# A four-layer decoder on one core: VectorE and ScalarE put into a written order from the local transformer to the end of the first cross attention

## The chip, the core and the metric

The kernel runs on one core of one Trainium2 chip. TensorE multiplies matrices into PSUM; VectorE, ScalarE and GpSimd (called POOL in the profile) do the work on elements; SyncE issues most transfers. Each engine takes its instructions in the order of its own queue, and an instruction waits until the semaphores of what it needs have come. The metric is the time of one execution on the device in microseconds (us).

## The reference

The model is a decoder with layernorm after each part (post-norm), over 32 sequences of 64 tokens with 128 features: 2048 tokens, `x` of shape (32, 64, 128). There are four layers, each with self attention, cross attention to a context of the same shape, and a feed-forward part. Everything is in fp32. Cut to the parts that matter:

```python
x = layernorm(x + L0_attn(x))            # 16 heads of 8, rotary positions
x = layernorm(x + L0_xattn(x, ctx))      # two-way cross attention with a gate
x = layernorm(x + L0_ffn(x))             # "local transformer", two layers:
    #   h = shift_token(t); q, k, v = h @ wqkv        (8 heads of 64)
    #   q, k = rotary(l2norm(q) * qs), rotary(l2norm(k) * ks)
    #   t = t + softmax(8 q k^T, causal) v @ wo
    #   h = layernorm(shift_token(t)) * g + b
    #   t = t + (a * gelu(g)) @ w2 + b2,  a, g = split(h @ w1 + b1)
x = layernorm(x + L1_attn(x))            # "latent attention": 16 heads of 64, k and v from 64 latents
x = layernorm(x + L1_xattn(ctx, x, ctx)) # first plain cross attention, 16 heads of 8
x = layernorm(x + L1_ffn(x))             # 8 experts, tokens sorted by expert
x = layernorm(x + L2_attn(x)); x = layernorm(x + L2_xattn(x, ctx))
x = layernorm(x + L2_ffn(x))             # 8 experts with room for 80 tokens each
x = layernorm(x + L3_attn(x)); x = layernorm(x + L3_xattn(x, ctx)); x = layernorm(x + fp8_linear(x))
```

## The kernel before

The tokens are four blocks (`NBLK`) of 512, each block four tiles (`TPB`) of 128 tokens, that is, of two sequences. `x` stays in SBUF through all layers.

**The table of steps.** Nothing runs in loops on the chip. Each stage enters small functions into a table, `sp.at(step, place, f)`; `Steps.run` sorts by step and place and calls them, and so the program is written out. A stage has a base step: local transformer 23, latent attention 55, first cross attention (`l1x`) 71, its experts' tiles from 92, second self attention (`l2a`) 96, second cross attention (`l2x`) 112. Stages overlap in steps: a tile that starts in step k is scored in step k + 2 and leaves in step k + 4, while the next stage's tiles start.

**Whose order holds.** TensorE always takes its instructions in the table's order (`manual_schedule`, at the end of `decoder_kernel`). In the stretches of steps in `sp.fixed` VectorE and ScalarE do so too. Everywhere else, and always for POOL and the transfers, a planner orders the instructions at compile time by dependences and by the times that it reckons. It also picks the buffers. Before the change the fixed stretches are the steps 95 to 128 and 136 to 196.

**PSUM.** Tag S has two buffers of two banks, for `qkps` (queries and keys before rotation) and `s64`/`s8` (scores). Tag G has four single banks, for all else: transposes `ropeT`, `ptps`, `hnT` and `xTps`, values `v64`, attention output `o64`, projection `y64`, the feed-forward's `gps`, `aps` and `y2`, the latents `latps`. A TensorE instruction that writes a bank waits until the bank's last reader, mostly a ScalarE copy, is done.

**A tile of heads of 64** (`tiles64`; local transformer with 8 heads, latent attention with 16) goes through these functions; the profile's names are in brackets:
- `start`: TensorE projects (qkps, v). In the local transformer ScalarE squares (sq, L1125), VectorE sums the squares (rn, L1129), and POOL takes max (L1130) and the power -1/2.
- `rope`: VectorE makes three products (turn) out of qkps, one of full and two of half size (`rope64`; in the latent attention twice three); POOL adds them and, in the local transformer, multiplies by rn.
- `rotate`, two steps later: TensorE transposes (ropeT, L969), ScalarE copies (qk, L970).
- `score`: scores (s); VectorE takes the maximum (mx, L988) and subtracts (p); ScalarE takes the exponential (p, L992).
- `normal`: VectorE sums (rec, L998) and inverts (L999); the multiplication of p is VectorE's for 8 heads and POOL's for 16.
- `probs`: transposes (ptps, L1009), copies (pT, L1011). `values`: TensorE (o), copies (oT, L1027). `out`: projection (y); for every second tile VectorE adds the residual (`done`).

Around them the local transformer has, for each block and layer: `shifted` (the shifted input hT; two ScalarE copies and a POOL memset), `normed` (copies xs, statistics, POOL's rstd, and VectorE centres xs, L1173), `turn_h`, `hidden` (three pairs gps/aps, Gelu on ScalarE, L1196, products on VectorE, L1197) and `second` (y2; two POOL additions resid in layer 1; acc on VectorE; in layer 1 the layernorm). Counted in steps from the block's first tile, `shifted` is at -1, `normed` to `second` are at 7, 8, 9 and 10, so each falls on a fixed one of a block's four steps. ScalarE loads a table of functions (ACT_TABLE_LOAD) before the first Gelu and again before the next exponential.

A layernorm is `moments` (statistics and aggregates on VectorE, rstd on POOL) and `normed`; with `pool=False`, as at the ends of the local transformer and the latent attention, VectorE makes nb = -mean * rstd (L522) and ScalarE applies it with four activations (x, L515).

**Routing** (`routed`) goes by pieces of tokens, in the last steps of a cross attention: `logits`, `compare`, `choose`, `chosen`, `rows` (ranks; inc in the profile) and one indirect POOL transfer per tile (L1362). Then `tables` finds which rows each expert tile takes and issues 23 loads on SyncE's queue; for the experts with limited room `loads` issues three.

Of the kernel before, what the change touches and what calls it, by code (L numbers as in the profile page):

```python
# [20 lines left out]
P = 128  # L21
# [260 lines left out]
class Decoder:  # L282
# [392 lines left out]
    def attn8(self, sp, base, name, src=None, rope=None, scale=1.0, row=None, mask=(None, None), has_out=True, split=False, number=False, turned=None, ahead=None, held=False):  # L675
# [142 lines left out]
        for blk in range(NBLK):  # L818
# [5 lines left out]
            if halved(blk):  # L824
                sp.at(*((base + 16, 6.5) if turned is None else (base + 16, 5.8)), lambda blk=blk: turn(blk, (0, 2)))
                sp.at(*((base + 17, 6.5) if turned is None else (base + 17, 2.1)), lambda blk=blk: turn(blk, (2, 2)))
                sp.at(*((base + 16, 6.4) if turned is None else (base + 16, 5.3)), lambda: normal_rest(0))
                sp.at(*((base + 17, 6.4) if turned is None else (base + 17, 2)), lambda: normal_rest(1))
# [5 lines left out]
        for n in range(4 * NBLK):  # L834
            sp.at(base + n, 0, lambda n=n: score(n))
            sp.at(base + n, 6.5 if held or ahead else 0.01, lambda n=n: exps(n))
# [135 lines left out]
    def scores64(self, qT, kT, nh):  # L972
# [18 lines left out]
        p3 = pr.rearrange("p n u k -> p (n u) k")  # L991
        nc.scalar.activation(p3, p3, AF.Exp)  # L992
        return p3
# [37 lines left out]
    def tiles64(self, sp, first, n, project, twist, turn, nh, wo, done):  # L1031
# [18 lines left out]

        def normal(i):
            self.normal64(st[i][0], nh)
# [20 lines left out]
        for i in range(n):  # L1073
            for lag, place, f in (
                (2, 0, rotate), (0, 1, start), (2, 2, score), (0, 2.3, rope), (2, 2.6, normal), (3, 4, probs), (4, 5, out),
                (3, 6, values),
            ):
                sp.at(first + i + lag, place, lambda f=f, i=i: f(i))


    def local_transformer(self, sp, base, names):

        nc = self.nc
        cur, tabs = {}, []
# [27 lines left out]
        def project(i):  # L1112
# [14 lines left out]
            nc.scalar.copy(v, vp)  # L1127
            rn = self.sb([P, 16], "rn", 3)
# [3 lines left out]
            return (ps, rn), (v[:, 0], v[:, 1])  # L1132

        def twist(i, t):
            ps, rn = t
            tab = tabs[i // 16]
            full = lambda a: a.unsqueeze(2).to_broadcast([P, 2, 8, 64])
            t1 = self.rope64(ps, full(tab[:, :, 0, :]), full(tab[:, :, 1, :]))
# [20 lines left out]
        def normed(l, blk):  # L1159
# [8 lines left out]
            for t in range(TPB):  # L1168
                nc.vector.bn_stats(st[:, t, :], xs[:, t, :])
                nc.vector.bn_aggr(mv[:, t, :], st[:, t, :])  # L1170
            r = self.rstd(mv[:, :, 1], TPB)
# [29 lines left out]
        def second(l, blk):  # L1201
# [13 lines left out]
            else:  # L1215
                self.norm(blk, x2, pool=False)
# [3 lines left out]
        for l in range(2):  # L1220
            for blk in range(NBLK):
                n = base + 16 * l + 4 * blk
                for lag, place, f in ((-1, 7, shifted), (7, 7, normed), (8, 7, turn_h), (9, 7, hidden), (10, 3, second)):
                    sp.at(n + lag, place, lambda f=f, l=l, blk=blk: f(l, blk))
                if l:
                    sp.at(n + 12, 3, lambda blk=blk: self.turn_x(blk))


    def latent_attn(self, sp, base, name):
# [3 lines left out]
        lats, zs = {}, {}  # L1233
# [44 lines left out]
        def done(i, y):  # L1278
# [5 lines left out]
            if t == TPB - 1:  # L1284
                self.norm(blk, zs.pop(blk), pool=False)

        self.tiles64(sp, base, 16, project, lambda i, t: t, turn, 8, lambda i: self.w[name]["wo"], done)
        for blk in range(NBLK):
            sp.at(base + 4 * blk - 1, 7, lambda blk=blk: latent(blk))
# [654 lines left out]
```

## Time and profile before

| | us |
|---|---|
| median of 3 runs (lowest, highest) | 1421.75 (1417.74, 1424.29) |
| profiled execution | 1411.89 |
| its span | 1410.1 |
| TensorE matmul busy | 1201.6 |
| VectorE busy | 931.4 |
| POOL busy | 741.2 |
| ScalarE busy | 688.2 |

In time the stages lie so: first attention and gated cross attention to about 147 us; local transformer's tiles from 147 to about 517; latent attention to about 800, with the last feed-forward parts of the local transformer in its first half; first cross attention to 885; experts to 945; the third layer to 1190; the last to the end. The profile gives busy time by engine, the waits (who waited for whom, in total, how often, and the longest), the chain (work followed back from the last instruction by what released it), and a timeline. PE is TensorE, DVE VectorE, ACT ScalarE; L346 and L343 are the helpers of all element-wise operations on two tensors and of all matmuls, so there the tensors' names tell which it is.

### The profile page before, as it was taken

Reading aid. Unit: us, or ns where it says so; the run is one execution under the profiler, and the core shown is the slowest. Engines: PE = TensorE matmul, PEld = TensorE weight load, DVE = VectorE, ACT = ScalarE, POOL = GpSimd, SP = SyncE. Lnnn points to the kernel's source line nnn. Section 1 sums busy time; section 2 is a strip of 40 time slices with the busy share of each in tenths; the row PEclk is TensorE's granted clock in tenths of the full one; section 3 lists DMA queues with packets and bytes.
Section 4 is the critical chain, followed back from the end, with each engine's and each line's share of the span. In section 5 each row is a group of like instructions: output and inputs, shape, how many; then the busy total and the mean of one; then the engine's idle time right before and its main releaser. Section 6 shows DMA issues by size and latency. Waiting matters only on the chain.

```text
span 1410.1 us, 37014 instructions
## 1 busy us (share of the span) xinstructions
PE 1201.6 (85%) x16009; PEld 870.3 (62%) x16009; DVE 931.4 (66%) x1852; ACT 688.2 (49%) x1176; POOL 741.2 (53%) x619
## 2 busy tenths in 40 slices
PE   7998877898888878998898998697999948889991
PEld 4775455565655555666667777584678847567770
DVE  6764667777876776766666576554668743766796
ACT  2453445555555535454545553463656524345562
POOL 3533688766876674544454245352355443336543
PEclk9999999999999889999999998697999868889995
DMA  6001010180010000010001100220001100000001
GB/s 240 3 2 26 1 47 1 36 265 2 1 55 1 1 1 2 2 69 2 2 1 35 36 2 29 70 86 16 10 3 48 37 14 23 9 9 3 3 2 30
DMA packets 33715, 43.16 MB, mean 31 GB/s; under 512 B 5946, under 2 KB 27121, under 8 KB 33168
## 3 DMA queue, kind: packets, MB, share of 16 engines
q1 hardware_dynamic: 31536, 38.20, 8.5%
q0 software_dynamic: 2016, 2.60, 0.6%
q8 instruction: 126, 2.06, 0.6%
q14 instruction: 37, 0.30, 0.1%
HBM read 26.63 MB, written 15.56 MB: 30 GB/s over the span
## 4 chain that ended last, share of the span: by engine, by line
PE 53%; DVE 20%; POOL 12%; ACT 9%; issue 4%; DMA 2%; SPq 0%; POOLq 0%; ACTq 0%; DVEq 0%
PE s L343 11%; PE o L343 9%; DVE turn L346 5%; PE qkps L343 5%; PE ptps L669 5%; PE proj L343 5%; POOL turn L346 5%; PE y L343 3%; PE ropeT L969 3%; ACT pT L671 2%; DVE rn L1129 2%; DVE p L346 2%; POOL rstd L346 2%; PE hps L343 2%; POOL rn L346 2%
## 5 line engine op out<-in xcount | busy, mean ns | idle before, releaser
L346 POOL TENSOR_TENSOR turn<-turn,turn 128x1024 f32<-128x1024 f32 x64 | 150.6, 2361 | 95.8 <-DVE turn L346 85.9
L656 DVE TENSOR_REDUCE mx<-s 128x16 f32<-128x1024 f32 x96 | 117.3, 1222 | 110.2 <-PE s L343 110.1
L346 DVE TENSOR_TENSOR p<-s,mx 128x1024 f32<-128x1024 f32 (+1 forms) x144 | 159.0, 1104 | 6.0
L671 ACT COPY pT<-ptps 128x512 f32<-128x512 f32 x192 | 103.5, 588 | 76.7 <-PE ptps L669 75.8
L726 ACT ACTIVATE p<-p 128x1024 f32<-128x1024 f32 x96 | 101.4, 1056 | 54.3 <-DVE p L346 54.1
L343 PE MATMUL s<-kx,q 32*64 32x128 f32 x3072 | 111.7, 284 | 7.4 <-DVE sparts L1725 3.7
L346 DVE TENSOR_TENSOR turn<-qkps,w_const 128x512 f32<-128x512 f32 (+1 forms) x96 | 75.9, 861 | 57.1 <-PE qkps L343 57.1
L440 POOL TENSOR_SCALAR rstd<-bnmv 128x4 f32<-128x4 f32 (+1 forms) x60 | 16.0, 266 | 183.8 <-DVE bnmv L489 158.1
L343 PEld LDWEIGHTS s<-kx,q 32*64 32x64 f32 x3072 | 87.6, 138 | 39.2 <-issue 33.3
L669 PE MATMUL ptps<-w_const,p 128*128 128x128 f32 x768 | 107.3, 284 | 0.7 <-ACT p L726 0.5
L969 PE MATMUL ropeT<-w_const,turn 128*128 128x128 f32 x512 | 70.2, 284 | 29.5 <-ACT oT L1027 12.6
L346 POOL TENSOR_TENSOR rn<-rn,nhalf 128x16 f32<-128x16 f32 x32 | 93.8, 2930 | 2.7
L669 PEld LDWEIGHTS ptps<-w_const,p 128*128 128x128 f32 x768 | 88.5, 146 | 9.9 <-issue 8.4
L594 POOL TENSOR_TENSOR kx<-k,w_const 128x1024 f32<-128x1024 f32 x31 | 59.1, 1927 | 65.5 <-ACT k L603 31.4
L343 PEld LDWEIGHTS o<-v,pT 128*64 128x64 f32 x2176 | 72.5, 139 | 32.3 <-ACT pT L671 16.0
L343 PE MATMUL o<-v,pT 128*64 128x18 f32 x2176 | 81.0, 214 | 5.4 <-ACT pT L671 4.2
L969 PEld LDWEIGHTS ropeT<-w_const,turn 128*128 128x128 f32 x512 | 58.5, 144 | 41.1 <-ACT oT L1027 11.8
L346 DVE TENSOR_TENSOR turn<-qkps,xtab 128x512 f32<-128x512 f32 (+1 forms) x96 | 82.0, 859 | 0.0
L343 PE MATMUL o<-pT,v 64*64 64x64 f32 x2048 | 71.6, 223 | 8.9 <-ACT pT L1011 8.9
L509 POOL TENSOR_SCALAR x<-z,bnmv,rstd 128x128 f32<-128x128 f32 x98 | 77.8, 806 | 2.5
L1129 DVE TENSOR_REDUCE rn<-sq 128x16 f32<-128x1024 f32 x32 | 39.0, 1217 | 57.6 <-ACT sq L1125 57.6
L343 PE MATMUL qkps<-wbig,hT 128*128 128x512 f32 x128 | 67.9, 657 | 10.4 <-POOL hT L1105 9.1
(345 smaller groups left out, 2791.3 us busy)
## 6 DMA issues: line engine op xcount, KB each, us to landing
sorted_x<-zero SPq DMA_DIRECT2D x9, 990.0 KB, 14.5
wbig<-in_l1f_w_dram SPq DMA_DIRECT2D x4, 1156.0 KB, 5.3
wbig<-in_l2f_w_dram SPq DMA_DIRECT2D x16, 256.0 KB, 2.8
wbig<-in_l0f_dram SPq DMA_DIRECT2D x2, 1561.0 KB, 8.5
z<-token_y SPq DMA_DIRECT2D x8, 256.0 KB, 2.8
wbig<-in_l1a_dram SPq DMA_DIRECT2D x1, 1856.0 KB
xsorted<-sorted_x SPq DMA_DIRECT2D x23, 66.0 KB, 1.8
xT<-in_xT_dram SPq DMA_DIRECT2D x4, 256.0 KB, 6.4
```

The lines of the kernel that those rows point to most:

```text
L343: self.nc.tensor.matmul(out, lhsT=lhsT, rhs=rhs, start=start, stop=stop)
L346: (eng or self.nc.vector).tensor_tensor(out=out, in0=a, in1=b, op=op)
L440: nc.gpsimd.tensor_scalar(r[:, :n], var, EPS, None, ALU.add)
L509: eng.tensor_scalar(x[:, t0 + t, :], z[:, t0 + t, :], mv[:, t, 0:1], r[:, t : t + 1], ALU.subtract, ALU.mult)
L594: self.wide = eng.tensor_tensor(out=kx, in0=bc(kT, 1, 2), in1=bc(head[:, 2 * i : 2 * i + 2], 2, TB), op=ALU.mult).ins
L656: nc.vector.tensor_reduce(mx, s3, AX.X, ALU.max)
L669: self.nc.tensor.transpose(ps[:, j, :], flat[:, c : c + P], self.ident)
L671: self.nc.scalar.copy(o, ps)
L726: nc.scalar.activation(prs[n], prs[n], AF.Exp)
L969: self.nc.tensor.transpose(pt[:, j * P : (j + 1) * P], f[:, j * P : (j + 1) * P], self.ident)
L1129: nc.vector.tensor_reduce(rn, sq, AX.X, ALU.add)
```

## The change

It adds the fixed stretch of steps 29 to 88, and lengthens the next by one step (95 to 129). The local transformer's first six steps (23 to 28) stay with the planner. In the new stretch VectorE and ScalarE follow the table, so the functions are given new places in a step and some are cut in two:
- `tiles64`: `normal` goes from the end of `score`'s step to place 0.5 of the next step; `rope` goes ahead of `score`; the exponential becomes a function of its own, `exps`, at 6.5, behind the copies of `values`.
- local transformer: rn (sum, max, power) moves from `project` into `twist`, behind the turn products. `normed` ends with rstd; the centring is a new function, `centred`, at 0.6 of the next step. The layernorm at the end of layer 1 splits into `moments`, in `second`, and `ended` at 6.6. The latent attention's layernorm splits the same way.
- first cross attention: the exponential goes to 6.5, where the later attentions have it. For both routed cross attentions the last half block's normalization and transpose go to 4.06 and 4.07, and the pieces of tokens 12 to 15 to other places. `tables` and `loads` go to place 0 of the step after.

TensorE's order changes only by this last point.

```diff
-                sp.at(*((base + 17, 6.5) if turned is None else (base + 17, 2.1)), lambda blk=blk: turn(blk, (2, 2)))
+                sp.at(*((base + 17, 4.07) if turned is None else (base + 17, 2.1)), lambda blk=blk: turn(blk, (2, 2)))
-                sp.at(*((base + 17, 6.4) if turned is None else (base + 17, 2)), lambda: normal_rest(1))
+                sp.at(*((base + 17, 4.06) if turned is None else (base + 17, 2)), lambda: normal_rest(1))
-            sp.at(base + n, 6.5 if held or ahead else 0.01, lambda n=n: exps(n))
+            sp.at(base + n, 6.5 if base else 0.01, lambda n=n: exps(n))
@@ scores64
-        p3 = pr.rearrange("p n u k -> p (n u) k")
-        nc.scalar.activation(p3, p3, AF.Exp)
-        return p3
+        return pr.rearrange("p n u k -> p (n u) k")
@@ tiles64
+        def exps(i):
+            nc = self.nc
+            nc.scalar.activation(st[i][0], st[i][0], AF.Exp)
-                (2, 0, rotate), (0, 1, start), (2, 2, score), (0, 2.3, rope), (2, 2.6, normal), (3, 4, probs), (4, 5, out),
-                (3, 6, values),
+                (2, 0, rotate), (3, 0.5, normal), (0, 1, start), (0, 1.5, rope), (2, 2, score), (3, 4, probs), (4, 5, out),
+                (3, 6, values), (2, 6.5, exps),
@@ local_transformer
+            return (ps, sq), (v[:, 0], v[:, 1])
+
+        def twist(i, t):
+            ps, sq = t
+            tab = tabs[i // 16]
+            full = lambda a: a.unsqueeze(2).to_broadcast([P, 2, 8, 64])
+            t1 = self.rope64(ps, full(tab[:, :, 0, :]), full(tab[:, :, 1, :]))
             rn = self.sb([P, 16], "rn", 3)
             nc.vector.tensor_reduce(rn, sq, AX.X, ALU.add)
             nc.gpsimd.tensor_scalar(rn, rn, 1e-24, None, ALU.max)
             self.tt(rn, rn, self.nhalf[:, 0:16], ALU.pow, nc.gpsimd)
...
-            r = self.rstd(mv[:, :, 1], TPB)
+            ff[l, blk] = xs, mv, self.rstd(mv[:, :, 1], TPB)
+
+        def centred(l, blk):
+            xs, mv, r = ff[l, blk]
             for t in range(TPB):
                 nc.vector.tensor_scalar(
...
-                self.norm(blk, x2, pool=False)
+                ends[blk] = x2, self.moments(blk, x2)
+
+        def ended(blk):
+            x2, moments = ends.pop(blk)
+            self.normed(blk, x2, moments, False)
...
-                for lag, place, f in ((-1, 7, shifted), (7, 7, normed), (8, 7, turn_h), (9, 7, hidden), (10, 3, second)):
+                for lag, place, f in ((-1, 7, shifted), (7, 7, normed), (8, 0.6, centred), (8, 7, turn_h), (9, 7, hidden), (10, 3, second)):
+                    sp.at(n + 10, 6.6, lambda blk=blk: ended(blk))
@@ latent_attn
-                self.norm(blk, zs.pop(blk), pool=False)
+                ends[blk] = self.moments(blk, zs[blk])
+
+        def ended(blk):
+            self.normed(blk, zs.pop(blk), ends.pop(blk), False)
+            sp.at(base + 4 * blk + 7, 6.6, lambda blk=blk: ended(blk))
@@ routed
-            (12, 2, [(n + 9, 4)], (n + 9, 4.05), (n + 9, 6), (n + 9, 6.1), (n + 9, 6.2), [(n + 9, 6.3)] * 2),
-            (14, 2, [(n + 9, 7)], (n + 9, 7.1), (n + 9, 7.2), (n + 9, 7.3), (n + 9, 7.4), [(n + 9, 7.5)] * 2),
+            (12, 2, [(n + 9, 4)], (n + 9, 4.05), (n + 9, 4.6), (n + 9, 4.7), (n + 9, 4.8), [(n + 9, 4.9)] * 2),
+            (14, 2, [(n + 9, 4.5)], (n + 9, 4.51), (n + 9, 7.2), (n + 9, 7.3), (n + 9, 7.4), [(n + 9, 7.5)] * 2),
@@ sorted_experts, capacity_experts
-        sp.at(ready + 9, 8.1, tables)
+        sp.at(ready + 10, 0, tables)
-        sp.at(ready + 9, 8.1, loads)
+        sp.at(ready + 10, 0, loads)
@@ decoder_kernel
+    sp.fixed.append((29, n + 18))
-    sp.fixed.append((n - 1, n + 33))
+    sp.fixed.append((n - 1, n + 34))
```

More of the change, by code (lines that the diff above doesn't have):

```diff
@@ L1083, in local_transformer @@
         nc = self.nc
-        cur, tabs = {}, []
+        cur, tabs, ends = {}, [], {}
         def tables():
@@ L1131, in project @@
             self.tt(rn, rn, self.nhalf[:, 0:16], ALU.pow, nc.gpsimd)
[L1132 to L1138, printed above, removed]
             self.tt(t1, t1, bc(rn, 2, 64), ALU.mult, nc.gpsimd)
@@ L1169, in normed @@
                 nc.vector.bn_stats(st[:, t, :], xs[:, t, :])
+            for t in range(TPB):
                 nc.vector.bn_aggr(mv[:, t, :], st[:, t, :])
-            r = self.rstd(mv[:, :, 1], TPB)
+            ff[l, blk] = xs, mv, self.rstd(mv[:, :, 1], TPB)
+        def centred(l, blk):
+            xs, mv, r = ff[l, blk]
             for t in range(TPB):
@@ L1232, in latent_attn @@
         tab = self.c["r1"].rearrange("p (c s d) -> p c s d", c=2, d=64)
-        lats, zs = {}, {}
+        lats, zs, ends = {}, {}, {}
         def latent(blk):
```

## The prediction

> **What bounds it now.** I read the span and busy shares first, then the windows by stage, then waits and the chain of the stages that the change touches, last the timeline engine by engine. The profiled execution took 1411.89 us (span 1410.1, 1.8 around it); it lies 9.9 below the median of the runs shown, 1421.75. I sum against 1411.9 and carry the difference over to the median.
>
> ```profile
> PE 1201.6 (85%) x16009; PEld 870.3 (62%) x16009; DVE 931.4 (66%) x1852; ACT 688.2 (49%) x1176; POOL 741.2 (53%) x619
> ```
>
> No engine is full, so waits between engines set the time. By windows, the local transformer (147 to 521 us) has TensorE busy 83 to 86%, the latent attention (521 to 800) 252 of 279 us, the steady part of the first cross attention (804 to 862) 55.4 of 58. What can be won lies in the first two.
>
> In the local transformer the longest waits (window 147 to 520; columns: us in total, times, longest) form a ring:
>
> ```profile
> POOL rn L1130 <- DVE rn L1129: 78.9, 27, 5.1
> ACT p L992 <- DVE p L346: 62.8, 28, 3.5
> DVE rn L1129 <- ACT sq L1125: 57.6, 25, 7.4
> ```
>
> The chain shows one turn of it (start us, us, what):
>
> ```profile
> 305.34 1.22 DVE rn L1129
> 306.56 1.13 DVE turn L346
> 307.69 0.60 DVE mx L988
> 308.29 0.60 DVE turn L346
> 308.88 0.61 DVE p L346
> 309.50 0.02 issue
> 309.52 0.06 ACT p L992
> 309.58 0.48 issue
> 310.05 0.58 ACT pT L1011
> 310.63 0.04 issue
> 310.68 1.15 PE o L343 x32
> 311.82 1.02 PE ropeT L969 x8
> 312.85 1.73 PE qkps L343 x4
> ```
>
> Before rn lie qkps (302.53, 1.73 us) and ScalarE's squares sq (304.28, 1.03 us), so a tile takes 10.32 us. ScalarE keeps the exponential (p) ahead of the copy pT of an older tile, so TensorE waits for this tile's scores to pass through VectorE, though `o` doesn't need them.
>
> In the latent attention a plain step is TensorE's own (673.7 to 686.4: 12.67 us, nearly without gaps). Time is lost where a layernorm ends (timeline of ScalarE, then of TensorE: start, us, what, and in brackets the idle time before it and what ended it):
>
> ```profile
> 701.36 1.65 ACT L515 ACTIVATE x<-z,nb,rstd 128x128 f32<-128x128 f32 x4 [3.43 <-DVE nb L522]
> 702.91 0.56 ACT L1239 COPY lat<-latps 128x512 f32<-128x512 f32 x1
> ```
> ```profile
> 703.53 1.11 PE L969 MATMUL ropeT<-w_const,turn 128*128 128x128 f32 x4 [3.86 <-ACT lat L1239]
> 704.44 3.62 PE L343 MATMUL qkps<-wbig,xT 128*128 128x512 f32 x4
> ```
>
> TensorE stands 3.86 us for a PSUM bank that `lat` must empty, and the next qkps takes 3.62 us where 1.88 is usual: it restarts slow. VectorE's nb took 1.86 us there (others 0.16), beside POOL's multiplication of p.
>
> **The change, part by part.** TensorE's order in the tiles stays as it was. A tile's VectorE order becomes: normalize the older tile (reduce 0.71, reciprocal 0.24, multiply 1.28 to 1.93, I take 1.70: 2.65), three turn products (2.33), rn (1.14), mx and p (1.20). ScalarE's exponential (0.65) is last in its step, and next step's normalizing waits for it. A **plain local step** so becomes a VectorE ring of 2.65 + 2.33 + 1.14 + 1.20 + 0.65 = 8.0 us instead of 10.3; TensorE needs 7.3, POOL about 8.1.
>
> But a block of four tiles has more. I count from the normalizing in the step that ends with `hidden`:
> - Ring to p 7.3, exponential 8.0, Gelu table 9.25, first Gelu 9.9; the third gps/aps pair waits for it, 11.9; last product 12.7. The next normalizing now stands behind these products; before, it ran while the table loaded.
> - Step with `second`: TensorE runs on from 11.8: ropeT 0.9, qkps 1.8, v 1.0, s 0.95, y2 2.8, ptps and its copy 1.2, o 1.15, then oT: 22.5. The exponential's table load follows oT (before, it lay in ScalarE's wait for p): 1.28, then 0.65: 24.4.
> - Step with `normed`: 2.65 + 4.67 = 31.8 at p; exponential and the two xs copies to 33.2, statistics and aggregates 34.5.
> - Step with `centred`: normalizing 37.1, and rstd (POOL, 1.35) is hidden behind it if POOL is free, or comes at 38.9 behind a turn product (2.25); centred 1.05, ring, exponential: 43.5 to 45.3.
> Mean 44.4. The starts of qkps give 46.5, 45.8, 44.1, 44.1 now, mean 45.1. So only 0.7 a block, **3 us** for the four and a half plain blocks: what the ring wins, the uncovered tables and the Gelu products take back.
>
> Here the Trainium skill speaks against the change. The profile has the load before an exponential as
>
> ```profile
> 618.37 1.28 ACT L992 ACT_TABLE_LOAD   x1 [4.07 <-DVE p L346]
> 619.66 1.06 ACT L992 ACTIVATE p<-p 128x1024 f32<-128x1024 f32 x1
> ```
>
> so the function starts 1.29 us after it. "ScalarE: Activation LUTs", section What ACT_TABLE_LOAD costs, puts a switch at about 2.66 us, 1.38 of them a drain. Eight loads come out of cover: 10.3 us by the row, which is in my sums, 21.3 by the rule; the gain would be 11 smaller. I take the row.
>
> **The two blocks with the second layer's norm** took 53.2 and 56.0. There acc waits for POOL's two resid (2.4), then rstd behind POOL's turn products; ScalarE stands 6.1 and 4.8 us at x. Now acc, statistics and rstd are issued at `second`, and nb and x after the exponential. VectorE's nb now waits in order, and behind it the normalizing; ptps waits for that. If resid is early, rstd is there at the exponential and 7 us are won each. If POOL puts pow (2.9) and resid ahead, acc comes 5 us later and ScalarE's qk copies after it, and 1 is won. I take 3.5 each: **7 us**.
>
> **Latent attention.** At the norms of its blocks 0 to 2: z, statistics, aggregates, rstd without POOL's multiplication beside it, nb at 697.9, oT, exponential until 698.95, x (1.55), lat done 701.0 in place of 703.5. TensorE's gap shrinks from 3.9 to 1.5 us and the slow restart (1.74 + 0.35) goes: 4.6 each, **14 us**. Against it: the exponential (1.06) now lies between oT and the qk copies. In steps where the bank of y is still held (three of four left) the last ropeT waits for the first copy, 0.9 us, five times uncovered: **-4.5**. In the steps with `second` (at 545 and 609) the table and the exponential come ahead of x: about 1 and 3 later: **-4**. Two waits for rstd before `centred` lose POOL's multiplication ahead of them: **+2**.
>
> **First cross attention.** Only its exponential moves (to the end of its step); TensorE is full: **-1**, between -4 and +2. In both routed tails the turn of the last half block goes ahead of the ranks of the tokens before it. Eight scatters at 1.27 us each on POOL's queue follow from 879.6 and end the stretch, whatever comes for the last pair: the first of them comes 0 to 0.5 us earlier each: **+0.5**. `tables` (23 loads on SP, and weight copies) and `loads` (three) move past no work; they only leave the ordered stretch, which in the second tail is one step longer now. Splitting exponential, norm and centring adds no instruction. DMAs and POOL stay under the planner.
>
> Sum: 3 + 7 + 14 - 4.5 - 4 + 2 - 1 + 0.5 = 17 us. 1411.9 - 17 = 1394.9 for a profiled execution, **1405** for the median. Its own range: 1397 to 1412.
>
> **Rivals.**
> *VectorE behind POOL* (slower). POOL's order is still the planner's, and VectorE can no longer step aside. It waits in order at eight centred, four acc and eight nb: twenty places. Local steps have POOL 8.1 busy of 8 to 11 us. If rstd always comes behind a turn product, the centred cost 11 more than my mean; if resid and pow go ahead at the four norms of the local transformer, 5 each, 20: 31 against the gain of 17, 1421.75 + 14 = 1436. It decides from 0.85 us a place. For it: POOL's chain ran resid, turn, turn, rstd at 444 to 452. Against: the latent norms find POOL idle.
> *The exponential in the way* (no change). If the late exponential holds ropeT in all sixteen latent steps, it costs 17 instead of 4.5: 1417; with the tables at 2.66, 1421 or more. Against: with four banks free, qk copies aren't waited for.
> *The ring opens* (more). POOL takes rstd and resid early everywhere: blocks at 43.5 (4 more in sum), norm blocks 7 each (7 more), `second` without loss (4): 1390.
>
> **Chances.** Forecast 0.45, POOL 0.23, exponential 0.19, ring 0.13. What a measurement can tell from no change is 0.5%, 7 us: 1414.6 to 1428.9. Faster: 0.45 + 0.13, and a little of the third, 0.60; slower 0.23; same 0.17. The range of 8 in 10: 1391 at the low end, where the ring's case starts, 1432 at the high end, in the middle of POOL's.
>
> **What would show it.** Right: in the local transformer turn directly after qkps and before rn; plain steps of 8 to 8.5 us; table loads of the exponential directly after oT; x at the latent norms some 2.5 us earlier, and qkps after it at 1.9, not 3.6 us. Wrong: long waits of VectorE for POOL's rstd or resid, more than 1 us each; ropeT waiting for qk copies in every latent step; slow qkps in places that had none. The stretches from 945 us on should keep their lengths.

## The result and the profile after

The changed kernel takes 1485.69 us (median; 1484.22 to 1486.62), the kernel before beside it 1421.22. The ratio is 1.0445, 95% interval 1.0403 to 1.0486: by that ratio **slower by 63 us**, where 1405 was forecast. The profiled execution has a span of 1484.4 us against 1410.1, 74.3 more; the profiled execution of before lay 9 us below its median, this one 0.6 above.

First, by the starts of TensorE's qkps and of POOL's scatters, where the 74.3 us are:

| stretch | before | after | more |
|---|---|---|---|
| start to the first tile of the local transformer | 147.1 | 149.5 | 2.5 |
| its first six steps (planner's order) | 64.0 | 70.2 | 6.2 |
| its seventh tile to the end of its tiles | 306.2 | 351.7 | 45.5 |
| latent attention, first to sixteenth tile | 230.7 | 231.5 | 0.7 |
| from there to the first scatter | 101.2 | 116.7 | 15.6 |
| the sixteen scatters of the first routing | 39.5 | 45.6 | 6.1 |
| all the rest | 521.5 | 519.2 | -2.3 |

The busy row of the changed kernel:

```profile
PE 1229.2 (83%) x16009; PEld 880.8 (59%) x16009; DVE 913.4 (62%) x1852; ACT 688.8 (46%) x1176; POOL 735.6 (50%) x619
```

VectorE and POOL are busy for less time than before (931.4 and 741.2); TensorE has 28 us more for the same instructions. So no engine has more to do: there is new waiting, and TensorE's work got slower around it. The waits of the changed kernel in the local transformer (window 147 to 571 us; us in total, times, longest):

```profile
POOL turn L346 <- DVE turn L346: 127.1, 26, 9.0
...
DVE turn L346 <- ACT sq L1127: 66.7, 31, 8.7
DVE acc L346 <- POOL resid L346: 40.8, 6, 7.7
...
PE ropeT L969 <- DVE acc L346: 34.4, 6, 6.6
...
PE qkps L343 <- POOL hT L1107: 25.6, 7, 4.9
```

The ring that I had shown (rn for sq, p for p) is gone from the top. In its place turn waits for the squares, and two small POOL operations hold TensorE: resid, which acc needs, and the memset of hT, which qkps needs. The same two waits of TensorE before (window 147 to 520):

```profile
PE qkps L343 <- POOL hT L1105: 9.1, 5, 3.0
...
PE ropeT L969 <- DVE acc L346: 1.3, 1, 1.3
```

The chain of the changed kernel passes through a step with `second` like this (start, us, what):

```profile
430.46 1.03 ACT sq L1127
...
431.51 2.43 DVE turn L346 x3
...
434.08 2.36 POOL turn L346
436.44 0.23 POOL rn L1139
...
436.74 2.93 POOL rn L346
...
439.75 1.90 POOL turn L346
441.65 1.06 POOL resid L346
...
442.74 0.70 DVE acc L346
...
443.48 1.12 PE ropeT L969 x4
```

Nothing in resid depends on this tile: it adds a row to x1, which was there three steps ago. It only stands in POOL's queue behind the four operations of this tile's rotation, 7.5 us. What TensorE sees of it, and of the memset a step later (timeline of TensorE; in brackets the idle time before, and what ended it):

```profile
443.48 1.12 PE L969 MATMUL ropeT<-w_const,turn 128*128 128x128 f32 x4 [5.29 <-DVE acc L346]
444.39 3.62 PE L343 MATMUL qkps<-wbig,hT 128*128 128x512 f32 x4
...
459.44 3.78 PE L343 MATMUL qkps<-wbig,hT 128*128 128x512 f32 x4 [3.02 <-POOL hT L1107]
```

The second half of ropeT needs the fourth G bank, which y2 holds until acc has read it. After these two gaps qkps takes 3.6 to 3.8 us instead of 1.88, after all thirteen such gaps 2.4 to 3.8. In the kernel before, POOL's order in the same places was (timeline of POOL):

```profile
396.84 2.93 POOL L346 TENSOR_TENSOR rn<-rn,nhalf 128x16 f32<-128x16 f32 x1
399.74 1.09 POOL L346 TENSOR_TENSOR resid<-x,w_rows 128x512 f32<-128x512 f32 x1
400.79 2.36 POOL L346 TENSOR_TENSOR turn<-turn,turn 128x1024 f32<-128x1024 f32 x1
...
410.34 2.36 POOL L346 TENSOR_TENSOR turn<-turn,turn 128x1024 f32<-128x1024 f32 x1 [0.25 <-DVE turn L346]
412.75 0.11 POOL L1105 MEMSET hT<- 64x8 f32 x1
412.94 2.06 POOL L346 TENSOR_TENSOR turn<-turn,rn 128x1024 f32<-128x1024 f32 x1
```

There resid lies between the power and the addition, in all six blocks that have one in this stage; the memset lies between the addition and the multiplication in five of seven places. In the changed kernel both lie behind all four operations, everywhere.

In the first cross attention the loss has another form. The chain at its start:

```profile
816.15 1.51 PE s L343 x34
...
817.68 1.24 DVE mx L656
818.94 1.23 DVE p L346
820.17 1.14 DVE rec L996
821.33 0.26 DVE rec L997
...
821.75 1.91 POOL p L346
...
823.71 1.97 PE ptps L1007 x8
```

L656 is the maximum of the new attention's scores, which TensorE makes first in this step; rec (L996) is the normalization of a latent tile that was scored in the step before. VectorE takes them in this order, because the scores are at place 0 and the normalization at 0.5. So the old tile's transposes (ptps), in the middle of the step, wait for the scores of the same step, and the next scores come behind the transposes. Three steps, from scores to scores, take 18.7, 15.9 and 16.2 us that took 15.7, 10.7 and 9.6.

### The profile page after: what moved, and what is told of

Same layout as the page of the kernel before. It is cut to its first block, busy times and chain, and to the rows that moved or that the text cites. A ratio compares the mean times of both kernels' runs of the same rounds, so it can differ in the third digit from the quotient of the medians.

```text
span 1484.4 us, 37063 instructions
## 1 busy us (share of the span) xinstructions
PE 1229.2 (83%) x16009; PEld 880.8 (59%) x16009; DVE 913.4 (62%) x1852; ACT 688.8 (46%) x1176; POOL 735.6 (50%) x619
## 4 chain that ended last, share of the span: by engine, by line
PE 51%; DVE 19%; POOL 13%; ACT 10%; issue 4%; DMA 2%; SPq 0%; POOLq 0%; ACTq 0%; DVEq 0%
PE s L343 10%; PE o L343 8%; DVE turn L346 6%; PE qkps L343 6%; POOL turn L346 5%; PE proj L343 5%; PE ptps L669 4%; PE y L343 4%; POOL rn L346 4%; PE ropeT L969 3%; ACT pT L671 2%; DVE p L346 2%; PE ptps L1007 2%; ACT sq L1127 2%; DVE mx L656 1%
## 5 line engine op out<-in xcount | busy, mean ns | idle before, releaser
L656 DVE TENSOR_REDUCE mx<-s 128x16 f32<-128x1024 f32 x96 | 117.3, 1222 | 131.1 <-PE s L343 124.9
L671 ACT COPY pT<-ptps 128x512 f32<-128x512 f32 x192 | 103.6, 588 | 74.4 <-PE ptps L669 73.4
L969 PE MATMUL ropeT<-w_const,turn 128*128 128x128 f32 x512 | 74.2, 291 | 54.6 <-DVE acc L346 34.4
L346 DVE TENSOR_TENSOR turn<-qkps,xtab 128x512 f32<-128x512 f32 (+1 forms) x96 | 77.5, 861 | 66.7 <-ACT sq L1127 66.7
L343 PE MATMUL qkps<-wbig,hT 128*128 128x512 f32 x128 | 84.5, 796 | 25.6 <-POOL hT L1107 25.6
L970 ACT COPY qk<-ropeT 128x512 f32<-128x512 f32 x128 | 67.5, 592 | 25.4 <-PE ropeT L969 25.2
L1009 ACT COPY pT<-ptps 128x512 f32<-128x512 f32 x68 | 38.7, 588 | 87.5 <-PE ptps L1007 87.5
```

Source lines behind the costliest of these rows:

```text
L343: self.nc.tensor.matmul(out, lhsT=lhsT, rhs=rhs, start=start, stop=stop)
L346: (eng or self.nc.vector).tensor_tensor(out=out, in0=a, in1=b, op=op)
L656: nc.vector.tensor_reduce(mx, s3, AX.X, ALU.max)
L671: self.nc.scalar.copy(o, ps)
L969: self.nc.tensor.transpose(pt[:, j * P : (j + 1) * P], f[:, j * P : (j + 1) * P], self.ident)
L970: self.nc.scalar.copy(dst, pt.rearrange("p (n t) -> p n t", t=P))
```

## The experiments

The runs stood on several chips; on them the kernel before took from 1406.8 to 1423.7 us. I therefore go by the ratio to the kernel before on the same chip, and turn it into time with 1421.2. The three stretches are those of the table above, from one profile each; in the two profiles of the same kernel, h4 and j0, they differ by 0.3, 5.1 and 4.3 us, so smaller differences between rows say nothing by themselves.

| run | ratio (95%) | local, from seventh tile | latent | to first scatter |
|---|---|---|---|---|
| before | 1 | 306.2 | 230.7 | 101.2 |
| changed | 1.0445 (1.0403-1.0486) | 351.7 | 231.5 | 116.7 |
| e1_resid_early | 1.0228 (1.0181-1.0275) | 312.6 | 232.6 | 118.2 |
| e2_hT_early | 1.0356 (1.0309-1.0404) | 338.2 | 231.0 | 117.8 |
| e3_norm_ahead | 1.0352 (1.0298-1.0406) | 351.6 | 231.5 | 102.9 |
| e4_all_three | 0.9999 (0.9972-1.0026) | 301.6 | 233.4 | 101.1 |
| g1_planner_local | 1.0546 (1.0501-1.0592) | 364.1 | 232.2 | 117.5 |
| g2_before_early | 0.9966 (0.9948-0.9984) | 298.3 | 230.6 | 101.2 |
| g3_norm_at_end | 1.0000 (0.9980-1.0020) | 298.0 | 232.2 | 104.1 |
| g4_tail_back | 1.0031 (1.0009-1.0053) | 299.3 | 232.3 | 100.8 |
| h1_rn_first | 1.0166 (1.0149-1.0183) | 319.5 | 228.2 | 117.8 |
| h2_before_rn_last | 1.0150 (1.0127-1.0173) | 321.9 | 231.4 | 102.4 |
| h3_before_places | 1.0239 (1.0222-1.0256) | 334.1 | 230.3 | 100.8 |
| h4_three_rn_first | 0.9883 (0.9845-0.9922) | 289.8 | 229.4 | 100.8 |
| i1_norm_at_end | 0.9926 (0.9896-0.9956) | 291.0 | 231.8 | 102.7 |
| i2_latent_exp_late (computes something else) | 0.9792 (0.9747-0.9837) | 292.7 | 214.3 | 97.6 |
| i4_planner_order | 1.0030 (1.0011-1.0049) | 306.4 | 230.0 | 100.8 |
| j1_latent_exp_late | 1.0063 (1.0042-1.0084) | 289.6 | 244.7 | 111.9 |
| j0_three_rn_first | 0.9878 (0.9833-0.9923) | 289.5 | 234.5 | 105.1 |

### First: take the suspected waits away, one by one

e1 writes POOL's two additions one step earlier:

```diff
+        def resided(l, blk):
+            xb = resids[l, blk] = self.residual(x1s.pop((l, blk)), self.rows[f"l0f_b2{l}"])
+            if l:
+                self.tt(xb, xb, cur[0, blk], ALU.add, nc.gpsimd)
...
-(9, 7, hidden), (10, 3, second)
+(9, 1.4, resided), (9, 7, hidden), (10, 3, second)
```

> The changed kernel with one edit: POOL's additions resid, which acc needs, are written one step earlier, ahead of that step's turn products. Theory P (POOL's order, which is not the table's, makes VectorE wait at acc, and TensorE's ropeT waits for the bank that acc empties): the waits of ropeT for acc, 34.4 us in the changed kernel, go, and with six of them the slow qkps after it (3.62 for 1.88 us, about 10 us): 1485.7 - 44 = 1441, between 1433 and 1450. Rival R (VectorE's ring is the bound because turn now stands behind ScalarE's squares, 66.7 us of waits; the wait at acc only takes up time that the ring would take anyway): no more than 10 us gained, 1475 or above.

Measured 1.0228, 1454 us: 31 us of the 63 come back. The waits of ropeT for acc are gone, the local stretch is 39 us shorter in its profile, but the time fell by less than the 44 us that I had put, and 1454 lies outside P's range. R is excluded.

e2 writes the memset (and the allocation of hT) at place 0.2 of its step:

```diff
+        def edged(l, blk):
+            h = hTs[l, blk] = self.q2([P, TB], "hT")
+            nc.gpsimd.memset(h[64:128, :].rearrange("p (b s) -> p b s", s=S)[:, :, 0:1], 0.0)
...
-for lag, place, f in ((-1, 7, shifted),
+for lag, place, f in ((-1, 0.2, edged), (-1, 7, shifted),
```

> The changed kernel with one edit: POOL's memset of hT is written at the beginning of its step instead of its end. Theory P: the waits of qkps for hT, 25.6 us, mostly go, with the slow qkps and v after them (about 11 us); since ScalarE's own copies into hT end some 2 us before the memset does, some 1 us a place stays: 1485.7 - 28 = 1458, between 1450 and 1468. Rival R (the ring through the squares is the bound): at most 8 gained, 1478 or above.

Measured 1.0356, 1472 us: 13 us come back, between the two. TensorE no longer waits for the memset, but the step with the Gelu, 13.2 to 13.7 us in the changed kernel, becomes 14.5 to 16: in a plain block the two steps around the memset win 4.6 us, and the step with the Gelu takes 2.3 of them back.

e3 moves the normalization ahead of place 0:

```diff
-                (2, 0, rotate), (3, 0.5, normal), (0, 1, start),
+                (2, 0, rotate), (3, -0.2, normal), (0, 1, start),
```

> The changed kernel with one edit: VectorE's normalization of the older tile is written at place -0.2 of its step instead of 0.5. In the local transformer and the latent attention VectorE's order stays the same; only in the three steps where the first cross attention starts (its scores are at place 0) does the normalization come ahead of the new scores' maximum. Theory C (there the last latent tiles wait in VectorE's order behind scores that come at the end of TensorE's step, a closed ring of 16 us a step): the 20.0 us that the first cross attention lost come back: 1466, between 1462 and 1471. Rival X (the loss there comes from its exponential, which the change moved to the end of the step): within 4 us of the changed kernel, 1482 or above.

Measured 1.0352, 1471 us. The stretch to the first scatter falls from 116.7 to 102.9 (101.2 before): the closed ring there is shown, at 14 us rather than 20. The sixteen scatters take 40.5 us in e3 and 45.6 in the changed kernel, but that isn't this edit: in e2, without it and on the same chip as e3, they take 40.5 as well.

e4 has all three:

> The changed kernel with all three edits. If they add: 1485.7 - 44 - 28 - 20 = 1394, between 1380 and 1412, that is below the kernel before (1421). Rival R (a ring of VectorE through the squares stands behind the POOL waits): 1440 or above.

Measured 0.9999: the kernel is where it was before the change. So the three edits give back **all of the 63 us**; one by one they give 31, 13 and 13, 57 in sum. But 1394 was wrong: the gain that I had forecast isn't underneath. Without the three waits the local stretch is 4.6 us shorter than before the change, where I had 10 (3 for the plain blocks, 7 for the two with a norm), and the latent attention isn't shorter (233.4), where I had 7.5 less. R, which wanted 1440 or more, is out as well.

### Whose fault is POOL's late order?

I had reasoned that POOL's planned order was harmless while VectorE could step aside, and that the written order took this away. g1 starts the written order behind the local transformer, with everything else changed:

```diff
-    sp.fixed.append((29, n + 18))
+    sp.fixed.append((55, n + 18))
```

> The changed kernel with one edit: the written order of VectorE and ScalarE begins at step 55 instead of 29, so the local transformer has the new places and split pieces but the planner's order. Theory P (the loss there is VectorE waiting in order for POOL): the local transformer's tiles end within 10 us of where they end before the change, the ropeT waits for acc fall below 10 us, and what is left is the 20 us at the start of the first cross attention: ratio to the kernel before 1.010 to 1.022. Rival E (the edits to the table lose the time themselves: rn behind the turn products, the exponential late): the local transformer stays at least 35 us longer, ratio 1.038 or above.

P fell and E held: 1.0546, slower than the changed kernel itself, with a local stretch 12 us longer. POOL and VectorE in it (timelines):

```profile
445.14 1.90 POOL L346 TENSOR_TENSOR turn<-turn,rn 128x1024 f32<-128x1024 f32 x1
447.00 1.09 POOL L346 TENSOR_TENSOR resid<-x,w_rows 128x512 f32<-128x512 f32 x1
```
```profile
448.12 0.69 DVE L346 TENSOR_TENSOR acc<-y,resid 128x512 f32<-128x512 f32 x1 [6.35 <-POOL resid L346]
```

The planner puts resid behind the rotation with or without the written order (POOL's sequence of these operations is the same in both kernels throughout), and VectorE under the planner waits as long, 40.8 us in sum. It is not the order of VectorE; it is what the edits of the table do to POOL's order.

g2 gives the early resid and memset (the diffs of e1 and e2) to the kernel before:

> The kernel before with the two POOL edits (resid a step earlier, memset of hT at the beginning of its step), all else as it was. Theory P (late POOL work costs only where VectorE can't step aside): the waits for it before are short (acc 8 us, qkps for hT 9 us in sum), so within 0.4% of the kernel before. Rival Q (the two edits are a gain of their own, whatever VectorE's order is): 12 us or more faster, ratio 0.991 or below.

0.9966: P as written, and a small gain of 5 us with the local stretch 8 shorter. Late small work of POOL costs little in the kernel before because there it isn't late.

Two parts of the change could have made it late. h1 undoes one, h2 and h3 put each alone into the kernel before:

```diff
@@ h1: rn back into project, in front of the turn products
+            rn = self.sb([P, 16], "rn", 3)
+            nc.vector.tensor_reduce(rn, sq, AX.X, ALU.add)
+            nc.gpsimd.tensor_scalar(rn, rn, 1e-24, None, ALU.max)
+            self.tt(rn, rn, self.nhalf[:, 0:16], ALU.pow, nc.gpsimd)
+            return (ps, rn), (v[:, 0], v[:, 1])
-            return (ps, sq), (v[:, 0], v[:, 1])
@@ h2: the same four lines taken from project into twist, in the kernel before
@@ h3: in the kernel before, exps as a function of its own, and
-(0, 1, start), (2, 2, score), (0, 2.3, rope), (2, 2.6, normal), (3, 4, probs), (4, 5, out), (3, 6, values),
+(3, 0.5, normal), (0, 1, start), (0, 1.5, rope), (2, 2, score), (3, 4, probs), (4, 5, out), (3, 6, values), (2, 6.5, exps),
```

> The changed kernel with one part undone: rn (VectorE's sum, POOL's maximum and power) is back in front of the turn products. Theory P2 (with rn behind the turn products POOL's addition, maximum, power and multiplication of a tile follow each other without a gap, and the planner puts resid and the memset of hT behind all four; in the kernel before they fit in while POOL waits for the turn products): the waits of ropeT for acc and of qkps for hT fall to a third or less, 30 us or more come back: ratio to the kernel before 1.023 or below. Rival E2 (the new places of normalization, rotation and exponential make POOL late): 1.038 or above.

> The kernel before with one part of the change alone: rn behind the turn products. VectorE and ScalarE stay with the planner. Theory P2: POOL's resid and memset come late here too, local transformer 30 to 45 us longer, ratio 1.020 to 1.035. Rival E2: within 0.7% of the kernel before.

> The kernel before with another part alone: the new places of rope, normal and the exponential in the tiles of 64, rn where it was, no written order. Theory P2: within 1% of the kernel before, with the waits for resid and hT no longer than there. Rival E2: 1.020 or above.

Neither theory was right alone. h1 gives 40 us back, as P2 had it, but the two waits of TensorE fall from 60.0 us only to 33.2, not to a third. h2 costs 21 (P2 wanted 28 or more, E2 at most 10), h3 costs 34 (E2). What POOL does in each, and the waits in the local transformer (from 147 us to the end of its tiles, us in sum; M is POOL's maximum, P the power, A the addition, X the multiplication of a tile, R resid, h the memset, a comma the border between two tiles):

| kernel | around resid | around the memset | acc for resid | ropeT for acc | qkps for hT |
|---|---|---|---|---|---|
| before | M P R A X | M P A h X (five of seven) | 8.2 | 1.3 | 9.1 |
| changed | A M P X, R | A M P X, h | 40.8 | 34.4 | 25.6 |
| g1, planner's order | A M P X, R | A M P X, h | 40.8 | 29.3 | 25.9 |
| h1, rn first | M P A R X | M P A X, h | 24.9 | 18.1 | 15.1 |
| h2, before with rn last | R A M P X | A M P X, h (six of seven) | 3.9 | 1.5 | 20.7 |
| h3, before with new places | M P A R X | M P A X, h | 24.8 | 17.1 | 22.5 |

Both parts disturb POOL. With rn last, addition, maximum, power and multiplication follow each other without a gap; with the new places and rn first, the turn products come so early that the addition stands at once behind the power. The timeline of POOL in h3:

```profile
420.49 2.93 POOL L346 TENSOR_TENSOR rn<-rn,nhalf 128x16 f32<-128x16 f32 x1
423.39 2.35 POOL L346 TENSOR_TENSOR turn<-turn,turn 128x1024 f32<-128x1024 f32 x1
425.70 1.10 POOL L346 TENSOR_TENSOR resid<-x,w_rows 128x512 f32<-128x512 f32 x1
```

Here resid is one place later than before the change, behind the addition, and one place earlier than in the changed kernel, in front of the multiplication. So go the waits of acc for resid: 8.2, 24.8 and 40.8 us. In h2 resid is early, and what waits is the centring for rstd (29.0 us in the same window, 15.8 before) and qkps for hT. By what rule the planner chooses these places is not shown; that the two edits of the table move them is.

h4 puts rn first into the kernel with all three edits:

> The kernel with all three edits, and rn back in front of the turn products. Theory V (VectorE's order is what a local step costs once POOL's small work is early; rn, 1.2 us, now stands in front of turn): 3 to 12 us slower than with the three edits, ratio 1.002 to 1.008. Rival L (POOL's chain of 7.5 us behind the turn products sets the pair of steps with the Gelu; the power could run beside the turn products): 6 us or more faster, ratio 0.996 or below.

L: 0.9883, and 0.9878 when it ran again:

> The kernel with the three edits and rn in front of the turn products once more, beside the run with the latent attention's exponential late, so that the two are compared on the same chip: 0.988 of the kernel before, between 0.984 and 0.994.

This version is **faster than both kernels**: 17 us, or 1.2%, under the kernel before (interval 11 to 24), 80 under the changed one. POOL in a step with `second` of it (j0):

```profile
393.98 2.93 POOL L346 TENSOR_TENSOR rn<-rn,nhalf 128x16 f32<-128x16 f32 x1
396.88 2.36 POOL L346 TENSOR_TENSOR turn<-turn,turn 128x1024 f32<-128x1024 f32 x1
399.32 1.90 POOL L346 TENSOR_TENSOR turn<-turn,rn 128x1024 f32<-128x1024 f32 x1
401.29 0.11 POOL L1098 MEMSET hT<- 64x8 f32 x1
```

The power runs beside the turn products, which VectorE makes from 393.48 to 395.8; in the chain of the changed kernel it starts at 436.74, 2.8 us after they end. The local stretch takes 290 us, 12 less than with rn last.

i4 takes the written order out of the local transformer of this version (the diff of g1):

> The same kernel, with the written order of VectorE and ScalarE from step 55 only; the local transformer goes to the planner. Theory O (with POOL's small work early the written order is a gain of its own, as it was 12 us with POOL late): local transformer 8 us or more longer than under the written order (290 us from its seventh tile), ratio 0.993 or above. Rival Z (only POOL's sequence counts): within 4 us, ratio 0.986 to 0.991.

O: 1.0030, local stretch 306.4 against 289.8. So with these places the written order is worth 17 us there, and with POOL late (g1 against the changed kernel) it was worth 12. **The part of the change that I had suspected is the part that gains.** Against the planner with its own places and the small work early (g2, 298.3) it is 8.5 us in this stretch.

### Smaller questions

g3 and i1 place the normalization at the end of the step before, ahead of the Gelu products:

```diff
-(3, -0.2, normal)
+(2, 6.8, normal)
```

> The kernel with all three edits, and the normalization written at 6.8 of the step before, ahead of the Gelu products and of the statistics instead of behind them. Theory H (the steps with the Gelu take 15 us because the normalization, 1.6 us, stands behind products that wait for ScalarE's table and Gelu): those steps fall to 13.5 us or less, six of them, 9 us, ratio to the kernel before 0.991 to 0.996. Rival K (the step with the Gelu and the one ahead of it keep their sum of 22.6 us, which POOL or TensorE sets): no change beyond 3 us against the kernel with the three edits, ratio 0.998 to 1.002.

> The kernel with the three edits and rn in front of the turn products (1407.8 us, 0.988 of the kernel before), and the normalization at 6.8 of the step before, ahead of the Gelu products. Theory H: the pair of steps around the Gelu (22.5 us in sum) loses the 1.6 us of the normalization: six pairs, up to 8 us, ratio 0.982 to 0.986. Rival K (TensorE's own work and the chain exponential, table, Gelu set the pair): within 0.3% of 0.988.

H falls both times: 1.0000 against 0.9999, and 0.9926 against the 0.9883 and 0.9878 of the same kernel without it, outside K's 0.3% on the slow side. In i1 the local stretch is 291.0 instead of 289.8; in g3 it is 298.0 instead of 301.6, but H wanted 9 less and the whole kernel is no faster. The normalization's place isn't what the pair of steps around the Gelu waits for.

g4 puts the routed tails back to their old places, in the kernel with all three edits:

> The kernel with all three edits, and the routed tails with their old places (the last half block's normalization and transpose at 6.4 and 6.5, the pieces of tokens 12 to 15 at 6 and 7). Theory S (with the new places POOL's copy of before comes behind six scatters, so the last two scatters come 3 us later): the gap in the train of eight scatters goes and the first tail is 2 us shorter; second tail within 1 us; ratio 0.997 to 1.000. Rival N (the new places win time in the second cross attention, 4 us between its first and last scatters): ratio 1.001 to 1.004.

1.0031, in N's range and outside S's, but the profiles don't decide it. The sixteen scatters take 40.0 us instead of 43.6 in e4 and 42.3 in g3, which ran on the same chip as g4; the rest of the kernel is 6.5 longer than in e4, of which 2.6 lie between the first and last scatters of the second routing, and it varies by 17 us over all these runs. The gap of 3.1 us in the train of the last eight scatters, which S was to explain, stays. POOL's timeline has its cause, before and in the changed kernel:

```profile
878.77 0.19 POOL L1337 COPY before<-before 128x8 f32<-128x8 f32 x1 [0.82 <-DVE slot L1407]
...
879.64 1.09 POOL L1362 DMA_INDIRECT sorted_x<-x,slot  x1 [0.55 <-DVE slot_f L1357]
```
```profile
960.84 0.96 POOL L1377 DMA_INDIRECT sorted_x<-x,slot  x1 [0.31 <-issue]
961.81 0.20 POOL L1352 COPY before<-before 128x8 f32<-128x8 f32 x1
...
963.96 0.98 POOL L1377 DMA_INDIRECT sorted_x<-x,slot  x1 [1.83 <-DVE size L1481]
```

Before, the copy of `before` stands ahead of all eight scatters, in the changed kernel behind six of them, as S had it; but in g4 it stands behind six too. Here again a small POOL instruction comes late. The places that g4 restores aren't what moves it; what does is open.

i2 and j1 ask why the latent attention gained nothing:

```diff
@@ i2
-(2, 6.5, exps),
+((2, 6.5) if nh == 4 else (3, 0.1)) + (exps,),
@@ j1
-(2, 0, rotate), (3, -0.2, normal), (0, 1, start)
+(2, 0 if nh == 4 else -0.5, rotate), (3, -0.2, normal), (0, 1, start)
-(2, 6.5, exps),
+((2, 6.5) if nh == 4 else (3, -0.3)) + (exps,),
```

> The same kernel, and in the latent attention alone the exponential behind the four qk copies of the next step instead of ahead of them. Theory T (the exponential's 1.06 us ahead of the copies holds the last ropeT; 0.8 to 0.9 us in each second step): the steps of 13.5 and 14.9 us in the second half of the latent attention fall to the 12.7 and 14.1 of the kernel before, 4 to 5 us in sum. Rival W (then the normalization, POOL's multiplication and ptps come late instead): the latent attention stays as long or gets longer.

In i2 the exponential of the latent attention came behind the normalization in the program, so it normalizes first and takes the exponential then, and nothing waits for the exponential but the transposes. Its 214.3 us are of another computation and settle nothing.

> The kernel with the three edits and rn in front of the turn products; in the latent attention alone the exponential stands behind the qk copies of the next step and ahead of the normalization. (The run before it had the normalization ahead of the exponential in the latent attention, so that it computed something else there; its time does not answer this.) Theory T (the exponential ahead of the copies holds the last ropeT): the steps of 13.5 and 14.9 us in the second half of the latent attention fall to 12.7 and 14.1; 3 to 6 us in sum against the 229.4 of the latent attention. Rival W (normalization, POOL's multiplication and ptps come late instead): the latent attention is 2 us or more longer.

W: 244.7 us, ten to fifteen longer than j0 and h4. Waits of j1 in the latent attention (560 to 760 us; in j0 the two are 34.7 and 7.9):

```profile
DVE rec L996 <- ACT p L1051: 67.5, 12, 8.0
...
PE s L343 <- DVE turn L346: 26.6, 12, 4.5
```

ropeT hardly waits for the copies any more (1.2 us, 6.2 in j0), but now VectorE stands in its order at rec, behind it the turn products, and TensorE's next scores need the S bank that turn empties. Of these two places the end of its own step is the better one.

## Why the prediction was wrong

**The step that failed** is the last one of the account: "DMAs and POOL stay under the planner", costed at nothing in the plain blocks, and with it "TensorE runs on from 11.8" through `second`. The planner's order of POOL didn't stay what it was. TensorE stood for it at 13 places, 60.0 us: six acc that waited up to 7.7 us for resid, and seven hT; e1 and e2 give 44 us of the kernel's time for them, with the slow qkps behind the gaps. A block of four plain tiles takes 53.9 us (tiles 8 to 24); I had 44.4, from 45.1. In numbers, "3 us for the plain blocks" was a loss of 38 in the same span. With POOL's small work early and rn last, which is the order that I had summed, a block takes 45.4 (e4), so even then my 44.4 was 1.0 too low and the gain of 0.7 isn't there. (The terms listed for the step with `second` add to 22.2, not 22.5; with that the mean would be 44.1.) With rn first (h4) it takes 44.4: the same number from another order, which is luck.

**The rival on the losing side** had the right engine and the right direction, and five faults of its own. It made the written order the cause (g1 and i4: the written order gains). It counted acc only where the second layer's norm is, though every `second` has one. It priced a late resid at 5 us, where the gap of TensorE and the slow qkps behind it make 7. Its waits for rstd, the most of its twenty places, didn't grow: 10.7 us at the centring and 3.0 at nb in this stage, 15.8 and 2.5 before. And the memset of hT, a 0.11 us instruction, stood in no list of what VectorE or TensorE waits for.

**The ring.** "Turn directly after qkps" was wrong: turn waits for the squares, 31 times, 66.7 us, and starts 0.02 to 0.03 us after them. Both read qkps in PSUM. The Trainium skill has this in "PSUM — Partial Sum Buffer", section PSUM bank collisions raise a hardware error: ScalarE and VectorE must not read one bank at once, and the compiler's scheduler adds a dependency between two such instructions. The trace agrees with the order, by the starts just given; that this is the reason no run here shows. With it rn behind turn gains nothing on VectorE (the squares are done when turn begins) and takes POOL's power out of the cover of the turn products: 12 us in the local stretch (e4 against h4).

**Multiplication of p.** I took 1.70 us as a mean of rows between 1.28 and 1.93. It is 0.69 in three of four steps and 2.2 to 2.3 in the step with `normed`, where it runs beside POOL's multiplication. This error was in my favour.

**Table loads.** Right: each lies directly behind oT, 1.28 us, and the exponential begins 1.30 after it (438.31 and 439.61). The 2.66 us of the Trainium skill's "ScalarE: Activation LUTs", section What ACT_TABLE_LOAD costs, did not show: I was right to take the row.

**Norm blocks** (last eight tiles of the local transformer): 7 won was forecast; it was 7.9 lost (112.0 for 104.1), and 10.8 won in h4. The condition that I had written, resid early or late, has a large part in it: with resid early alone (e1) they take 100.6.

**Latent attention**: 7.5 won was forecast; 0.7 was lost. The mechanism at the norms was right. Timeline of ScalarE, then of TensorE, for the place shown before:

```profile
755.94 1.06 ACT L1051 ACTIVATE p<-p 128x1024 f32<-128x1024 f32 x1
756.90 1.64 ACT L515 ACTIVATE x<-z,nb,rstd 128x128 f32<-128x128 f32 x4
758.44 0.57 ACT L1250 COPY lat<-latps 128x512 f32<-128x512 f32 x1
```
```profile
759.06 0.66 PE L969 MATMUL ropeT<-w_const,turn 128*128 128x128 f32 x4 [1.28 <-ACT lat L1250]
759.55 1.88 PE L343 MATMUL qkps<-wbig,xT 128*128 128x512 f32 x4
```

The gap is 1.28 (I had 1.5), qkps 1.88, and the two steps there win 3.9 of 4.6. But `latent` of a next block, which holds the bank, exists only at two of the three norms, and at the other of the two 2.4 is won: 6.3 for 14. Against it the ropeT waits cost 0.8 to 0.9 as forecast, but at two plain steps; the two steps with `second` cost 1.0 and 1.1, not 4 together; and "+2" at the centring was **3.8 lost** in one step: there VectorE centres for 2.81 us ahead of the turn products, and TensorE's mask product waits 2.86 us for the bank.

**First cross attention**: "TensorE is full: -1" was 15.6 lost. I had looked at the steady part and not at the three steps in which two attentions share VectorE; e3 shows it. **Routed tails**: +0.5 was a loss of 6.1 in the first. Of it 1.9 is the gap behind POOL's late copy; the rest isn't taken apart, and this stretch takes 39.5 to 48.6 us over the runs that have the old tail. **Behind the last of these scatters** the length kept within 2.3 us, about as forecast from 945 us on. The 8.7 us that were lost ahead of the seventh tile, for which the forecast had no term, aren't taken apart either.

## What to carry to other kernels

When some engines get a written order and one stays with a planner, list every small instruction of the planned engine that a written one waits for, look again at where the planner puts it after each edit of the table, and write it into the table early; their own duration (0.11 and 1.1 us here) says nothing of what they hold up. Where two stages overlap, check the order of each shared engine in the overlapping steps, not only in the steady ones. And before a reduction is moved behind the work that it used to overlap, ask what long instruction on another engine it starts: here a 1.2 us sum started a 2.9 us power.

## What was not expected of the hardware

A gap of TensorE need not be long to make the next product slow. In the changed kernel a qkps took 3.78 us after 3.02 us idle, and the v after it 1.98 instead of 1.08; after 5.29 us and a ropeT it took 3.62, after 1.28 us and a ropeT 1.88. In the kernel before, after 2.21 to 2.23 us and a ropeT, it took 1.88 three times, and after 2.26 us 3.36, so these traces give no sharp length. The granted clock over the local stretch (windows) was 0.91, against 0.96 before and 0.97 in j0, so a gap is paid for twice.
